# Layer 0's first keys ahead of other transfers, x loaded later, and unread products on TensorE at the start

## The chip, the cores and the metric

The kernel runs on one core of one Trainium2 chip. The metric is the device time of one execution in microseconds (us); the median of several executions is compared. Five engines work side by side and meet through semaphores: TensorE (PE, with its weight loads as PEld), VectorE (DVE), ScalarE (ACT), GpSimd (POOL) and SyncE (SP). Each engine runs its own queue in order. Loads are issued by instructions in the queues of SP and ACT and are carried out by 16 DMA engines.

## The reference

Four layers of a small transformer work on 32 sequences of 64 tokens of width 128, with a context of the same shape. Each layer adds a cross-attention block and a feed-forward block. Only layer 0's attention matters here. Cut to its core, with the context as the images and the normalised x as the latents:

```python
# x, ctx: (32, 64, 128); 16 heads of 64
img = layer_norm(ctx, ln1_g, ln1_b)
lat = layer_norm(layernorm(x), ln2_g, ln2_b)
q = lat @ Wq                                 # 64 queries a sequence
k, v = split(concat([img, lat]) @ Wkv)       # 128 keys a sequence
x = x + softmax(q @ k.T / 8) @ v @ Wo        # by head
```

After it come layer 0's feed-forward block with dequantised weights, and layers 1 to 3, which the change leaves as they are.

## The kernel before, in words

Layer 0's attention never forms the queries, keys and values. For each of the 16 heads it forms `A = Wq Wk^T / 8` (128x128) and `N = Wv Wo`. Then a sequence needs its 128 normalised tokens `kv_tok` (64 of the context, 64 of x, on the 128 partitions), their transpose `kvT`, the projection `G = A^T lat` (`l0_project`), scores `G kvT` with their softmax, the product with the tokens (`Ct`) and the sum over heads of `Ct N`, which is added to x.

The 32 sequences are taken as eight "quarters" `q` of four sequences (GT = 4). The change's title calls `q == 2` the third quarter. `l0_load` loads the tokens of one `q`: the context's half on SP's queue, x's half on ACT's. `l0_inputs` makes the keys: statistics (`ln_moments`, the helper's lines 154 and 155), a power on POOL (`rsqrt`, line 161), the normalisation (`ln_apply`, line 183), the gain (line 403) and the offset (line 404), four transposes (line 408), the copy to `kvT` (line 409), and two splits into a rounded part and its rest (`split`, lines 213 and 218): `latT_hi` and `latT_lo` of the latents' half of `kvT`, `tokp_hi` and `tokp_lo` of the tokens. Three rounded products in place of one (`mm3`, line 236) keep the precision.

`l0_products` multiplies pairs of weights for eight heads at a time (a half `hf`); `take_A` writes `A_hi` on ACT (line 364) and `A_lo` on DVE (line 365). `l0_project` multiplies `A` with `latT` for two heads per step `n`; the steps 0 to 3 need the half `hf = 0` only. `l0_unit` is one of 64 units: scores (line 445), maximum `nm` (line 447), exponentials, the normalisation on POOL (line 461), transposes (line 465), the split (468, 469), the product with the tokens, and for the last unit of a pair of sequences the sum over heads (479) and the addition to x (480). A unit of `q` also projects a step of `q + 1`, loads `q + 2` at its step 0 and makes its keys at step 2.

At the start the kernel loads quarter 0's tokens, WqT and WkT by halves, `gains`, quarter 1's tokens, WvT and Wo, then x in four groups of 256 KB (`K.x[g]`) and `cols`, a table of small bias columns. The first user of `cols` is `half_cols` (line 299), a scaled copy made by `later_constants`, which also makes `identb` and the mask `pair_mask`. The weights of the middle blocks are loaded by the task `mid_weights`, interleaved with the units.

The order in the text of the program is a priority only. The launch asks for a schedule made with a simulated timeline (`schedule_with_timeline_sim=True`): each engine's queue is laid out ahead of the run from simulated times, and on the chip it is worked off in that order, whatever arrives late. Two helpers restrict it: `in_turn(K, [a, b])` puts b behind a on their engine without waiting for a to end, and `tc.issue_after(a)` does the same for all that a block of the program issues on a's engine. A tile's buffer is used again when its readers are done: `kv_tok` has two buffers, so the load of quarter 2 waits for quarter 0's readers.

`keep_warm` issues products that nobody reads. Before the change it is called late in the kernel only, with the rounded identity `identb` as weights and a mask of the later layers, `K.masks[1]`, as the moving operand.

Of the kernel before, what the change touches and what calls it, by code (L numbers as in the profile page):

```python
# [4 lines left out]


# [3 lines left out]

# [8 lines left out]
F32 = mybir.dt.float32  # L19
F32R = mybir.dt.float32r  # L20
BF16 = mybir.dt.bfloat16
# [125 lines left out]
def ln_moments(K, pool, xg, own=""):  # L147

    nc = K.nc
    n = xg.shape[1]  # L150
    st = pool.tile([P, n, 6], F32, name="ln_st")
    mv = pool.tile([P, n, 2], F32, name=f"ln_mv{own}")
    for t in range(n):
        nc.vector.bn_stats(st[:, t, :], xg[:, t, :])
        nc.vector.bn_aggr(mv[:, t, :], st[:, t, :])
    return mv
# [51 lines left out]
def split(K, pool, src, name, engine=None, bufs=None, after=None):  # L208

    nc = K.nc  # L210
    hi = pool.tile(list(src.shape), F32R, name=f"{name}_hi", bufs=bufs)
    lo = pool.tile(list(src.shape), F32R, name=f"{name}_lo", bufs=bufs)
    first = nc.scalar.copy(hi, src) if isinstance(K, Later) else nc.vector.tensor_copy(hi, src)
    if after:
        in_turn(K, [after, first])
    if not isinstance(K, Later):
        K.mark = first
    (engine or nc.gpsimd).tensor_tensor(lo, src, hi.bitcast(F32), ALU.subtract)
    return hi, lo


# [61 lines left out]
def constants(K, pool):  # L283

    nc = K.nc
    K.ident = pool.tile([P, P], F32, name="ident")
    make_identity(nc, K.ident)
    K.neghalf = pool.tile([P, 1], F32, name="neghalf")
    nc.vector.memset(K.neghalf, -0.5)


def later_constants(K, pool):
    nc = K.nc
    K.identb = pool.tile([P, P], BF16, name="identb")
    nc.vector.tensor_copy(K.identb, K.ident)
    K.identr = pool.tile([P, P], F32R, name="identr")
    nc.vector.tensor_copy(K.identr, K.ident)
    K.half = pool.tile([P, NCOL], F32, name="half_cols")
    nc.vector.tensor_scalar(K.half, K.cols, 0.5, None, ALU.mult)

    K.pair_mask = pool.tile([P, GT, P], BF16, name="pair_mask")
    nc.vector.memset(K.pair_mask, NEG)
    for b in range(2):
        nc.vector.memset(K.pair_mask[b * S : (b + 1) * S, :, b * S : (b + 1) * S], 0.0)

    K.rank = pool.tile([P, 8], F32, name="rank")
    for e in range(8):
        nc.vector.memset(K.rank[:, e : e + 1], float(8 - e))
# [7 lines left out]
N_TAGS = "2n"  # L316


def l0_products(K, out, left, right, hf, tags=("s", "t")):


    ps = [bank(K, tag, [P, 4, P]) for tag in tags]
    for j in range(4):
        for r in range(2):
            rows = slice(r * S, (r + 1) * S)
            K.nc.tensor.matmul(ps[r][:, j, :], left[rows, 4 * hf + j, :], right[rows, 4 * hf + j, :], start=True, stop=True)
    for r in range(2):
        out(ps[r], hf, r)


def l0_xattn(K):


    nc, tc, ins = K.nc, K.tc, K.ins
    with (
        tc.tile_pool(name="l0x_w", bufs=1, reuse_waits="tile") as wp,
        tc.tile_pool(name="l0x_g", bufs=2, reuse_waits="tile") as gp,
        tc.tile_pool(name="l0x_t", bufs=L0_BUFS, reuse_waits="tile") as tp,
    ):
        C = SimpleNamespace(gp=gp, tp=tp, tok={}, keys={}, G={})  # L340

        C.A = tuple(wp.tile([P, 16, P], F32R, name=f"A_{n}") for n in ("hi", "lo"))
        C.N = wp.tile([P, 16, P], F32, name="N")
        with tc.tile_pool(name="first", bufs=1, side="right", reuse_waits="tile") as first:
            l0_load(K, C, 0)
            w = {n: first.tile([P, 8, P], F32, name=n) for n in ("WqT", "WkT", "WvT", "Wo")}
            from_dram = {n: ins[f"L0_xattn_{n}"].rearrange("(c p) d -> p c d", p=P) for n in w}
            half = [slice(4 * hf, 4 * hf + 4) for hf in range(2)]
            gains = wp.tile([P, 2, P], F32, name="gains")
            K.kv_gamma, K.kv_beta = gains[:, 0, :], gains[:, 1, :]  # L350
            for hf in range(2):
                nc.sync.dma_start(w["WqT"][:, half[hf], :], from_dram["WqT"][:, half[hf], :])
                nc.scalar.dma_start(w["WkT"][:, half[hf], :], from_dram["WkT"][:, half[hf], :])
                if hf == 0:
                    nc.sync.dma_start(gains, ins["gains"])
            l0_load(K, C, 1)
            nc.sync.dma_start(w["WvT"], from_dram["WvT"])
            nc.scalar.dma_start(w["Wo"], from_dram["Wo"])
            heads = lambda t, hf, r: t.rearrange("p (c r) d -> p r c d", r=2)[:, r, half[hf], :]

            def take_A(ps, hf, r):
                hi, lo = (heads(a, hf, r) for a in C.A)
                scale = 1.0 / math.sqrt(64.0)
                nc.scalar.activation(hi, ps, AF.Copy, scale=scale)
                nc.vector.scalar_tensor_tensor(lo, ps, scale, hi.bitcast(F32), ALU.mult, ALU.subtract)

            l0_inputs(K, C, 0)
            for hf in range(2):
                l0_products(K, take_A, w["WqT"], w["WkT"], hf)
                for n in range(4 * hf, 4 * hf + 4):  # L370
                    l0_project(K, C, 0, n, "gn"[n % 2])
            l0_inputs(K, C, 1)

            with tc.issue_after(K.projected.ins):
                for hf in range(2):
                    l0_products(K, lambda ps, hf, r: nc.scalar.copy(heads(C.N, hf, r), ps), w["WvT"], w["Wo"], hf, N_TAGS)
        for g in range(NG):
            K.x[g] = K.load(K.const, f"x{g}", [P, GT, P], K.tokens(ins["x"], g))
        K.cols = K.load(K.const, "cols", [P, NCOL], ins["cols"])
        mid_begin(K)  # L380
        units = [(q, t, hf, b) for q in range(8) for t in range(2) for hf in range(2) for b in range(2)]
        interleave(K, (Task(l0_unit(K, C, *u)) for u in units), L0_DEPTH, L0_LAG, L0_RATE)


def l0_load(K, C, q):
    tok = C.tok[q] = C.gp.tile([P, GT, P], F32, name="kv_tok")
    for rows, name, queue in ((slice(0, S), "ctx_1024", K.nc.sync), (slice(S, P), "x", K.nc.scalar)):
        batches = K.ins[name].rearrange("(b s) d -> s b d", s=S)
        queue.dma_start(tok[rows, :, :], batches[:, GT * q : GT * (q + 1), :])


def l0_inputs(K, C, q):

    nc, gp = K.nc, C.gp
    tok = C.tok[q]
    mv = ln_moments(K, gp, tok)
    rs = gp.tile([P, GT], F32, name="ln_rs")
    nc.vector.tensor_scalar(rs[0:S, :], mv[0:S, :, 1], EPS, None, ALU.add)
    nc.vector.tensor_scalar(rs[S:P, :], mv[S:P, :, 1], 1.0 + EPS, EPS * EPS, ALU.mult, ALU.add)
    ln_apply(K, tok, tok, mv, rsqrt(K, gp, rs, "ln_rstd"))  # L400
    full = [P, GT, P]
    engine = nc.vector if q == 0 else nc.gpsimd
    engine.tensor_tensor(tok, tok, K.kv_gamma.unsqueeze(1).to_broadcast(full), ALU.mult)
    engine.tensor_tensor(tok, tok, K.kv_beta.unsqueeze(1).to_broadcast(full), ALU.add)
    kvT = gp.tile(full, F32, name="kvT", bufs=3)
    ps = bank(K, "1", full)
    for b in range(GT):
        nc.tensor.transpose(ps[:, b, :], tok[:, b, :], K.ident)
    nc.scalar.copy(kvT, ps)
    latp = split(K, gp, kvT[:, :, S : 2 * S], "latT", nc.vector)  # L410
    tokp = split(K, gp, tok, "tokp", bufs=3)
    C.keys[q] = (kvT, latp, tokp)

# [14 lines left out]
def l0_unit(K, C, q, t, hf, b):  # L428
# [5 lines left out]
    G = C.G[q]  # L434
    if n == 0 and q + 2 < 8:
        l0_load(K, C, q + 2)
    if n == 2 and q + 2 < 8:
        l0_inputs(K, C, q + 2)
    if (hf, b) == (0, 0):
# [604 lines left out]
HEAD_BLOCKS = ("L2", "L3")  # L1044
WARM = ((0, 0, 0, 0), (0, 0, 2, 4))
WARM_END = 2


def heads_constants(K, pool):
# [318 lines left out]
def keep_warm(K, ps, n, after=None):  # L1368

    cols = ps.shape[-1]  # L1370
    moving = K.masks[1].rearrange("p h k -> p (h k)") if len(K.masks[1].shape) == 3 else K.masks[1]
    for _ in range(n):
        step = K.nc.tensor.matmul(ps, K.identb, moving[:, :cols], start=True, stop=True)
        if after is not None:
            in_turn(K, [after, step])
        after = step
    return after


def in_turn(K, steps):  # L1380

    for a, b in zip(steps, steps[1:]):
        order = mybir.DependencyInfo(mybir.DependencyClass.NoSync, mybir.DependencyReason.DATA)
        K.tc.add_manual_dep(b.ins, a.ins.name, order, reason="order of issue")
# [354 lines left out]
```

## Time and profile before

| | us |
|---|---|
| median of 3 runs | 907.39 |
| lowest and highest | 906.65 and 907.55 |
| the profiled execution | 907.62 |
| its span, first to last instruction | 905.9 |

| engine | busy us | share of the span |
|---|---|---|
| PE | 821.4 | 91% |
| PEld | 671.2 | 74% |
| DVE | 732.4 | 81% |
| ACT | 563.0 | 62% |
| POOL | 328.3 | 36% |

The mean granted TensorE clock of the execution is 0.98. In the timeline a row has the start and the duration in us, the engine, the line of the kernel, the operation, what it writes and reads, and the number of instructions merged into the row; in square brackets stands the idle time of the engine ahead of it and what ended that. A row of several instructions that overlap in a pipeline lasts less than their sum. Rows of "SPq" and "ACTq" are the queue of an engine: the issue of a load. Layer 0's attention takes the span from the start to about 320 us (its last sum over heads, line 479, starts at 319.5), with the middle blocks' groups between its units.

### The profile page before, as it was taken

What the parts mean: (1) busy time and instruction counts of PE and PEld (TensorE: products, weight loads), DVE (VectorE), ACT (ScalarE), POOL (GpSimd) and SP (SyncE); (2) the same over time, 40 slices, a digit from 0 to 9 for tenths busy, and PEclk for the clock granted to TensorE, in tenths of its full rate; (3) what the DMA queues carried; (4) which work ended last, traced back from release to release, by engine and by line L of the source; (5) the groups of instructions that cost most, each with busy time, mean ns of one, the idle gap of its engine ahead of it and who ended that gap; (6) DMA issues with size and microseconds to landing.
All of it is one profiled execution on the core that took longest, in us unless ns stands there. A gap on an engine that the chain in (4) does not pass through costs nothing.

```text
span 905.9 us, 15766 instructions
## 1 busy us (share of the span) xinstructions
PE 821.4 (91%) x5859; PEld 671.2 (74%) x5868; DVE 732.4 (81%) x1877; ACT 563.0 (62%) x1093; POOL 328.3 (36%) x300
## 2 busy tenths in 40 slices
PE   4999999999999988899999799898999779898995
PEld 3989989979988876787787688684676447566663
DVE  5879799798698687877678877789788778789878
ACT  3676685676676599587687768564544484345443
POOL 3764574343243251511040310015474303435342
PEclk9999999999999999999999999999999999899998
DMA  8312000000000000000000000000000000000000
GB/s 191 106 36 59 13 2 12 13 1 1 13 1 1 1 13 0 15 14 21 1 1 1 1 1 1 0 25 1 1 2 1 1 1 1 1 1 1 13 13 24
DMA packets 22670, 13.73 MB, mean 15 GB/s; under 512 B 3009, under 2 KB 21953, under 8 KB 22593
## 3 DMA queue, kind: packets, MB, share of 16 engines
q1 hardware_dynamic: 18320, 10.62, 4.3%
q10 hardware_dynamic: 4272, 2.10, 0.9%
q8 instruction: 46, 0.75, 0.3%
q14 instruction: 32, 0.25, 0.1%
HBM read 11.66 MB, written 1.05 MB: 14 GB/s over the span
## 4 chain that ended last, share of the span: by engine, by line
PE 50%; DVE 25%; ACT 15%; POOL 3%; issue 3%; DMA 2%; SPq 1%; ACTq 0%; DVEq 0%; POOLq 0%
PE c_ps L918 7%; PE g_ps L479 4%; PE s_ps L1263 4%; PE s_ps L445 4%; PE g_ps L236 4%; PE c_ps L236 3%; PE g_ps L1283 2%; PE c_ps L1273 2%; PE s_ps L236 2%; PE t_ps L465 2%; PE t_ps L236 2%; ACT L941 2%; DVE mh_lo L895 1%; ACT L936 1%; DVE m L893 1%
## 5 line engine op out<-in xcount | busy, mean ns | idle before, releaser
L461 POOL TENSOR_TENSOR e<-e,rs 128x512 f32<-128x512 f32 x64 | 67.0, 1058 | 91.7 <-DVE rs L460 52.8
L161 POOL TENSOR_TENSOR ln_rstd<-ln_rs,neghalf 128x4 f32<-128x4 f32 (+1 forms) x38 | 40.8, 1073 | 144.8 <-DVE ln_rs L169 137.5
L1249 POOL TENSOR_TENSOR kb<-hk,head 128x1024 f32<-128x1024 f32 x32 | 63.7, 1993 | 74.2 <-PE s_ps L1263 58.9
L445 PE MATMUL s_ps<-kvT,G 128*128 128x128 f32 x512 | 71.7, 277 | 0.5 <-DVE e L451 0.5
L1263 PE MATMUL s_ps<-kb,hq 128*128 128x512 f32 x128 | 67.3, 609 | 2.1 <-ACT hq L1232 1.9
L445 PEld LDWEIGHTS s_ps<-kvT,G 128*128 128x128 f32 x512 | 65.8, 192 | 4.1 <-DVE e L451 1.9
L918 PE MATMUL c_ps<-mh_hi,w2e_hi 128*128 128x512 f32 x160 | 61.8, 426 | 4.5 <-ACT be L936 2.7
L479 PE MATMUL g_ps<-N,Ct 128*128 128x128 f32 x512 | 62.1, 276 | 1.1 <-ACT G L425 0.7
L479 PEld LDWEIGHTS g_ps<-N,Ct 128*128 128x128 f32 x512 | 60.1, 192 | 2.5 <-ACT G L425 1.3
L1266 ACT ACTIVATE e<-e 128x1024 f32<-128x1024 f32 x32 | 34.0, 1061 | 40.6 <-DVE e L1265 38.1
L1264 DVE TENSOR_REDUCE nm<-s_ps 128x8 f32<-128x512 f32 x64 | 43.7, 683 | 16.0 <-PE s_ps L1263 15.6
L1274 ACT COPY hpT<-c_ps 128x512 f32<-128x512 f32 x64 | 35.1, 589 | 34.2 <-PE c_ps L1273 33.9
L469 DVE TENSOR_TENSOR pT_lo<-t_ps,pT_hi 128x512 fp32r<-128x512 f32 x64 | 43.4, 683 | 13.5 <-ACT pT_hi L468 11.3
L918 PE MATMUL c_ps<-mh_hi,w2e_lo 128*128 128x512 f32 x160 | 51.9, 401 | 0.0
L895 DVE TENSOR_TENSOR mh_lo<-m,mh_hi 128x1024 fp32r<-128x1024 f32 x32 | 40.4, 1263 | 13.9 <-ACT mh_hi L894 12.9
L473 ACT COPY Ct<-c_ps 128x512 f32<-128x512 f32 x64 | 38.4, 600 | 21.2 <-PE c_ps L236 16.4
L918 PE MATMUL c_ps<-mh_lo,w2e_hi 128*128 128x512 f32 x160 | 49.4, 404 | 0.5 <-DVE mh_lo L895 0.5
L425 ACT COPY G<-g_ps 128x512 f32<-128x512 f32 x60 | 35.9, 598 | 21.4 <-PE g_ps L236 18.0
L452 ACT ACTIVATE e<-e 128x512 f32<-128x512 f32 x56 | 35.4, 638 | 20.8 <-DVE e L451 20.5
L1283 PEld LDWEIGHTS g_ps<-hv,hpT 128*64 128x64 f32 x1024 | 33.5, 137 | 19.3 <-issue 7.4
L447 DVE TENSOR_REDUCE nm<-s_ps 128x4 f32<-128x512 f32 x64 | 42.9, 679 | 5.0 <-PE s_ps L445 4.7
L468 ACT CAST pT_hi<-t_ps 128x512 fp32r<-128x512 f32 x64 | 38.1, 598 | 13.3 <-PE t_ps L465 7.3
(524 smaller groups left out, 2651.8 us busy)
## 6 DMA issues: line engine op xcount, KB each, us to landing
kv_tok<-in_x ACTq DMA_DIRECT2D x8, 128.0 KB, 3.3
kv_tok<-in_ctx SPq DMA_DIRECT2D x8, 128.0 KB, 2.9
x<-in_x SPq DMA_DIRECT2D x4, 256.0 KB, 8.3
ctx<-in_ctx SPq DMA_DIRECT2D x4, 256.0 KB, 3.4
w2e_raw<-in_L_ffn_expert_w SPq DMA_DIRECT2D x1, 768.0 KB, 4.4
out<-x SPq DMA_DIRECT2D x3, 256.0 KB, 2.3
WkT<-in_L_xattn_WkT ACTq DMA_DIRECT2D x2, 256.0 KB, 5.3
WqT<-in_L_xattn_WqT SPq DMA_DIRECT2D x2, 256.0 KB, 5.2
```

The costliest lines, as they stand in the source:

```text
L236: step = K.nc.tensor.matmul(ps, w[a], x[b], start=start and i == 0, stop=stop and i == 2)
L445: nc.tensor.matmul(ps[:, j, :], G[:, bb, h : h + 2, :].rearrange("p h s -> p (h s)"), kvT[:, bb, :], start=True, stop=True)
L447: K.mark = nc.vector.tensor_reduce(nm, ps, AX.X, ALU.max, negate=True)
L461: nc.gpsimd.tensor_tensor(e, e, rs.unsqueeze(2).to_broadcast([P, 4, P]), ALU.mult)
L469: nc.vector.tensor_tensor(lo, ps, hi.bitcast(F32), ALU.subtract)
L479: nc.tensor.matmul(ps, Ct[:, h, :], C.N[:, h, :], start=(h == 0), stop=(h == 15))
L895: nc.vector.tensor_tensor(lo, m, hi.bitcast(F32), ALU.subtract)
L918: nc.tensor.matmul(ps, K.w2p[part][:, 2 * n + i, cols], x[:, i, :, :], start=first, stop=last)
L1249: step = nc.gpsimd.tensor_tensor(kb, K.hk[C.i][g][:, :, t, :].unsqueeze(2).to_broadcast(full), K.head.unsqueeze(1).unsqueeze(3).to_broadca ...
L1263: nc.tensor.matmul(ps, hq[:, half, t, :, :].rearrange("p b s -> p (b s)"), kb[:, half, :, :], start=False, stop=True)
L1264: nc.vector.tensor_reduce(nm[:, heads], ps, AX.X, ALU.max, negate=True)
L1283: values = nc.tensor.matmul(po[b * S : (b + 1) * S, j, :, :].rearrange("p r d -> p (r d)"), pT[:, j, b * S : (b + 1) * S], K.hv[g][:, 2 * ...
```

## The change

- `identb` and `pair_mask` are made by `constants`, at the start, instead of `later_constants`.
- Eight unread products (128x512) are issued on TensorE behind the start of the first load in the program's text, and six more in turn behind the first half of the `A` products. `keep_warm` now takes `pair_mask` as its moving operand everywhere.
- The first half of the `A` products stands ahead of quarter 0's inputs in the text; the second half is put, on PE's queue, behind quarter 0's transposes (`K.turn0`).
- Quarter 1's statistics, and `half_cols`, are put on DVE's queue behind quarter 0's `latT_lo` (`K.lat0`).
- `cols` is loaded ahead of WvT.
- The x part of quarter 2's load is issued on SP, like the context's.
- The four loads of x are issued on SP behind quarter 2's load, inside the first unit.

```diff
@@ split
-    (engine or nc.gpsimd).tensor_tensor(lo, src, hi.bitcast(F32), ALU.subtract)
+    K.split_end = (engine or nc.gpsimd).tensor_tensor(lo, src, hi.bitcast(F32), ALU.subtract)
@@ constants (moved here from later_constants)
+    K.identb = pool.tile([P, P], BF16, name="identb")
+    nc.vector.tensor_copy(K.identb, K.ident)
+    K.pair_mask = pool.tile([P, GT, P], BF16, name="pair_mask")
...
@@ later_constants
-    nc.vector.tensor_scalar(K.half, K.cols, 0.5, None, ALU.mult)
+    in_turn(K, [K.lat0, nc.vector.tensor_scalar(K.half, K.cols, 0.5, None, ALU.mult)])
@@ l0_products
+            step = K.nc.tensor.matmul(...)
+            if after is not None:
+                in_turn(K, [after, step])
...
+    return step
@@ l0_xattn
             l0_load(K, C, 0)
+            keep_warm(K, bank(K, "1", [P, 512]), WARM_START)
...
             l0_load(K, C, 1)
+            K.cols = K.load(K.const, "cols", [P, NCOL], ins["cols"])
             nc.sync.dma_start(w["WvT"], from_dram["WvT"])
...
+            step = l0_products(K, take_A, w["WqT"], w["WkT"], 0)
+            keep_warm(K, bank(K, "g", [P, 512]), 6, step)
             l0_inputs(K, C, 0)
             for hf in range(2):
-                l0_products(K, take_A, w["WqT"], w["WkT"], hf)
+                if hf:
+                    l0_products(K, take_A, w["WqT"], w["WkT"], hf, after=K.turn0)
                 for n in range(4 * hf, 4 * hf + 4):
                     l0_project(K, C, 0, n, "gn"[n % 2])
...
-        for g in range(NG):
-            K.x[g] = K.load(K.const, f"x{g}", [P, GT, P], K.tokens(ins["x"], g))
-        K.cols = K.load(K.const, "cols", [P, NCOL], ins["cols"])
@@ l0_load
-        queue.dma_start(tok[rows, :, :], batches[:, GT * q : GT * (q + 1), :])
+        K.tok_step = (queue if q != 2 else K.nc.sync).dma_start(tok[rows, :, :], batches[:, GT * q : GT * (q + 1), :])
@@ l0_inputs
-    mv = ln_moments(K, gp, tok)
+    with K.tc.issue_after(K.lat0.ins) if q == 1 else nullcontext():
+        mv = ln_moments(K, gp, tok)
...
-        nc.tensor.transpose(ps[:, b, :], tok[:, b, :], K.ident)
+        turn = nc.tensor.transpose(ps[:, b, :], tok[:, b, :], K.ident)
...
+    if q == 0:
+        K.turn0, K.lat0 = turn, K.split_end
@@ l0_unit
         l0_load(K, C, q + 2)
+        if q == 0:
+            for g in range(NG):
+                x = K.x[g] = K.const.tile([P, GT, P], F32, name=f"x{g}")
+                in_turn(K, [K.tok_step, K.nc.sync.dma_start(x, K.tokens(K.ins["x"], g))])
@@
+WARM_START = 8
@@ keep_warm
-    moving = K.masks[1].rearrange("p h k -> p (h k)") if len(K.masks[1].shape) == 3 else K.masks[1]
+    moving = K.pair_mask.rearrange("p t k -> p (t k)")
```

More of the change, by code (lines that the diff above doesn't have):

```diff
@@ L7 @@
 import math
-from contextlib import ExitStack
+from contextlib import ExitStack, nullcontext
 from types import SimpleNamespace
@@ L287, in constants @@
     make_identity(nc, K.ident)
+    K.identb = pool.tile([P, P], BF16, name="identb")
+    nc.vector.tensor_copy(K.identb, K.ident)
+    K.pair_mask = pool.tile([P, GT, P], BF16, name="pair_mask")
+    nc.vector.memset(K.pair_mask, NEG)
+    for b in range(2):
+        nc.vector.memset(K.pair_mask[b * S : (b + 1) * S, :, b * S : (b + 1) * S], 0.0)
     K.neghalf = pool.tile([P, 1], F32, name="neghalf")
@@ L293, in later_constants @@
     nc = K.nc
-    K.identb = pool.tile([P, P], BF16, name="identb")
-    nc.vector.tensor_copy(K.identb, K.ident)
     K.identr = pool.tile([P, P], F32R, name="identr")
@@ L298, in later_constants @@
     K.half = pool.tile([P, NCOL], F32, name="half_cols")
[L299 to L304, printed above, removed]
+    in_turn(K, [K.lat0, nc.vector.tensor_scalar(K.half, K.cols, 0.5, None, ALU.mult)])
     K.rank = pool.tile([P, 8], F32, name="rank")
@@ L316, with l0_products @@
 N_TAGS = "2n"
-def l0_products(K, out, left, right, hf, tags=("s", "t")):
+def l0_products(K, out, left, right, hf, tags=("s", "t"), after=None):
     ps = [bank(K, tag, [P, 4, P]) for tag in tags]
@@ L325, in l0_products @@
             rows = slice(r * S, (r + 1) * S)
-            K.nc.tensor.matmul(ps[r][:, j, :], left[rows, 4 * hf + j, :], right[rows, 4 * hf + j, :], start=True, stop=True)
+            step = K.nc.tensor.matmul(ps[r][:, j, :], left[rows, 4 * hf + j, :], right[rows, 4 * hf + j, :], start=True, stop=True)
+            if after is not None:
+                in_turn(K, [after, step])
     for r in range(2):
         out(ps[r], hf, r)
+    return step
 def l0_xattn(K):
```

## The prediction

> **What bounds the kernel now.** I read the page first (TensorE busy in 91% of the span, VectorE in 81%, and the chain that ended last running mostly through TensorE). Nothing in the change touches work after layer 0's first quarter, so I went on to the view of busy time by stretches:
>
> ```profile
> 5.00:10.00 5.00, 2.88 (x23) 2.65 (x25) 3.01 (x15) 4.28 (x5) 1.02 (x1) 1.00 1.18 281
> 10.00:15.00 5.00, 2.36 (x16) 1.70 (x14) 2.83 (x11) 1.23 (x3) 0.00 (x0) 1.00 1.22 271
> 15.00:20.00 5.00, 1.75 (x6) 1.46 (x7) 3.79 (x13) 0.64 (x2) 3.26 (x3) 1.00 0.56 119
> 20.00:25.00 5.00, 5.00 (x25) 4.88 (x24) 2.56 (x12) 2.00 (x4) 3.76 (x4) 1.00 0.19 50
> 25.00:30.00 5.00, 5.00 (x38) 4.60 (x37) 4.25 (x12) 2.54 (x5) 3.28 (x4) 1.00 0.19 56
> 30.00:35.00 5.00, 5.00 (x41) 4.81 (x42) 4.51 (x16) 4.25 (x15) 3.34 (x4) 1.00 0.37 100
> ...
> 100.00:150.00 50.00, 48.86 (x381) 45.54 (x381) 44.81 (x116) 31.90 (x64) 25.36 (x22) 1.00 0.04 12
> ```
>
> The columns are stretch and length, then busy us of PE, PEld, DVE, ACT and POOL, the granted clock, DMA share and GB/s. From 20 us on PE is full, with DVE at 90% behind it (44.81 of 50 at 100 to 150 us). Before 20 us nothing is full but the DMA (share above 1 from 5 to 15 us). So the program is a long stretch at the rate of PE and DVE behind a start of 18 us; what shortens the start should shorten the whole. Next, VectorE's rows in order of time:
>
> ```profile
> 8.55 0.69 DVE L403 TENSOR_TENSOR kv_tok<-kv_tok,gains 128x512 f32<-128x512 f32 x1
> 12.17 0.87 DVE L154 BATCH_NORM_STATS2 ln_st<-kv_tok 128x6 f32<-128x128 f32 x4 [2.93 <-DMA kv_tok<-in_ctx]
> 12.96 0.67 DVE L404 TENSOR_TENSOR kv_tok<-kv_tok,gains 128x512 f32<-128x512 f32 x1
> ...
> 17.50 0.19 DVE L299 TENSOR_SCALAR half_cols<-cols 128x49 f32<-128x49 f32 x1 [0.51 <-DMA cols<-in_cols]
> 17.61 0.28 DVE L213 CAST latT_hi<-kvT 128x256 fp32r<-128x256 f32 x1
> 17.97 1.12 DVE L183 TENSOR_SCALAR kv_tok<-kv_tok,ln_mv,ln_rstd 128x128 f32<-128x128 f32 x4
> 18.99 0.42 DVE L218 TENSOR_TENSOR latT_lo<-kvT,latT_hi 128x256 fp32r<-128x256 f32 x1
> 21.45 0.87 DVE L154 BATCH_NORM_STATS2 ln_st<-kv_tok 128x6 f32<-128x128 f32 x4 [2.03 <-DMA kv_tok<-in_ctx]
> ```
>
> Quarter 0 needs only its beta addition (L404) before its transposes, but the statistics of quarter 1 stand ahead of it in the queue and wait 2.93 us for their tokens. Its keys (`kvT`) are copied by 15.44 us, but the cast to `latT_hi` stands behind both hf=1 `A_lo` and `half_cols`, which waits for `cols`; SyncE issued that only at 12.84, behind the four x loads, whose issue took from 6.30 to 12.80. Last, TensorE's rows:
>
> ```profile
> 17.95 0.58 PE L236 MATMUL g_ps<-latT_hi,A_hi 128*128 128x256 f32 x1 [3.13 <-DVE latT_hi L213]
> 20.28 0.41 PE L236 MATMUL g_ps<-latT_lo,A_hi 128*128 128x256 f32 x1
> 20.49 0.41 PE L236 MATMUL n_ps<-latT_lo,A_hi 128*128 128x256 f32 x1
> 25.38 0.41 PE L236 MATMUL n_ps<-latT_hi,A_lo 128*128 128x256 f32 x1
> 27.75 0.28 PE L236 MATMUL g_ps<-latT_lo,A_hi 128*128 128x256 f32 x1
> 27.86 0.28 PE L236 MATMUL g_ps<-latT_hi,A_hi 128*128 128x256 f32 x1
> ```
>
> The first projection starts at 17.95. Until about 25.7 like products start 0.21 us apart (20.28 to 20.49), afterwards 0.12 (27.75 to 27.86), while the granted clock reads 1.00 throughout: a second, slower rate that this column does not show. It ended 7.75 us after the stream began, 6.2 us after its last gap (before 19.47).
>
> **Part by part.** Quarter 0's keys. With quarter 1's statistics ordered behind `latT_lo`, L404 follows L403 at 9.24 and ends at 9.91 instead of 13.63: 3.7 us. Ahead of the transposes now stand the warm-up products. The like row of the trace (L1373, 128x512 bf16) shows 0.38 us for one and about 0.22 from start to start at the fast rate, so about 0.43 at the slow one. Eight from 3.4 us (`identb` is cast at 3.15 to 3.38) end at 6.85, costing the hf=0 products 0.4 us against 6.42; these keep their 2.1 us to about 8.9; six more end at 10.2 to 11.4, by the rate. The transposes thus start between 9.98 (tokens) and 11.4; I take 10.7, where the rate changes on the way. They take 0.66 (row at 31.00) to 1.12 us (row at 13.70), the copy 0.6, the cast 0.28: the first projection starts at about 12.4 (11.5 to 13.1) instead of 17.95. Gain 5.5 us.
>
> Before it DVE has room for the hf=0 `A_lo` (two of 0.66) and `tokp_hi` (0.41) between 9.91 and 12.0. The hf=1 products (about 1 us fast, 2.1 slow) go behind the transposes and delay the projection little, since it waits for the copy and cast; their `A_lo` go behind `latT_lo` as well as I read the queue.
>
> The slow rate. PE is now fed from 3.4 us on, so by the trace's 6.2 to 7.75 us it is fast from 9.6 to 11.2, before the first projection. Before, 17.95 to 25.7 was run slow, less a gap of 0.3: 7.4 us of work that takes 3.7 fast. The edit so offers PE 5.5 + 3.7 = 9.2 us.
>
> [...]
>
> DVE's share. The projection feeds units at 2.5 us of DVE each (four passes of some 0.6 apart), against 2.2 to 2.8 on PE, so DVE must follow. Between 9.24 and 40 us its idle rows sum to 7.9 us: 2.93 + 0.51 + 2.03 + 0.91 + 0.72 + 0.41 + 0.39. What remains after the change: about 0.5 waiting for `kvT`, some 2 on POOL's powers (1.02 to 1.25 each, rows L161) and quarter 2's tokens. POOL's two-operand passes now lie on different DVE rows: `latT_lo` took 0.42 alone and 1.45 beside L403, so another 0 to 1 us. That leaves 7.9 - 2.5 - 0.5 = about 5, with 4.4 to 5.4 as its ends. PE offers 9.2 and DVE 5; they alternate as the limit at 30 to 60 us (4.97 of DVE's 5.00 at 40 to 45, PE's full 5.00 at 30 to 40). I take 6.5.
>
> Loads. Without the x loads (1 MB) in the DMA between 6 and 13 us, quarter 1's tokens land before the 12.1 of now, and they are first wanted at 12.5. `cols` now precedes `WvT` on SyncE: one issue of 0.83, hidden since `WvT` is first read at 25.87 before, about 16 after. The x loads stand behind quarter 2's load, which waits for quarter 0's tile (`tokp_lo`, 1.3 us on POOL, to about 13.5). They then block SyncE for 1.7 us (four of 0.43) to 6.5; queued behind are quarter 3's load, which cannot start until quarter 1's tile is free at about 20 us (25.59 before), and the middle blocks' weights, which in the trace began at 32.38. x is first read in the addition at 59.73, so 8 us of landing is covered; without that cover each late us would be paid. The third quarter's ACT issue (0.60 us, behind an ACT wait of 2.95 in the row at 18.39) goes to SyncE: nothing was due on ACT then, but with the `G` copies early it would stand before them, so this keeps 0 to 3 us from being lost and adds no gain of its own. The mask read by the late warm-up products is another tile of the same shape: 0.
>
> Sum: the profiled execution took 907.62 us, its span 905.9 and 1.7 around it, 0.2 above the median 907.39. 907.6 - 6.5 = 901.1.
>
> **Rivals.** *PE alone counts*: DVE's queue is laid out anew and its waits close up; the whole 9.2 comes, less 0.5 for late units: 898.9; with the slow rate's end at its earliest and quarter 2's waits gone, 897. For it: PE at 5.00 from 20 to 40 us. Against: DVE's 4.97 after. *DVE takes it back*: two-operand contention and quarter 2's waits return, leaving about 3 (5 less the 2.03 now waited at 21.45): 904.6. *Hidden anyway*: the gain meets a date that does not move, such as the middle blocks' weights, whose chain (loads, casts, splits) runs from 39 to 75 us; layer 0's later units wait there, and less than 1.8 us remains: 907. Against: PE lost only 1.1 us from 40 to 60. *Slower*: the queues are laid out by a planner with simulated times, so POOL's place for the split of `w1e` may come before `e` products that PE needs. Now POOL waits 2.15 us for its DMA at 40.9. If layer 0 moves 6.5 earlier and this load, behind the x loads on SyncE, does not, the wait grows to 8.7; it decides above 6.5 us of growth, where PE has no other unit left. With a further 2.15 for the next raw tile (`w2e`): 909.5. Against: the load waits for layer 0's own buffers, which come free earlier too.
>
> **How the numbers follow.** My sum 0.46 (899.5 to 903.5 by its terms), PE alone 0.16, DVE 0.19, hidden 0.08, slower 0.11. A measurement tells about 0.2%, 1.8 us, from no change: the first three lie past it, so faster 0.81, same 0.08, slower 0.11. The range 896.5 to 906.3 leaves out the slower case, most of the hidden one and little at the lower end.
>
> **What would show it.** Right: no idle before L404, `latT_hi` cast before 13 us and the first L236 product at 11.5 to 13.1; products 0.12 apart from the first; the first `nm` reduction well before 30.16; PE's full stretches beginning by 13 us. Wrong: the first L236 after 15 us, or still 0.21 apart; ACT or DVE idle behind `WvT`, x or `cols`; or an early start with PE waiting for DVE between 15 and 60 us by more than 3 us.

## Result: the start is 6 us shorter, the whole no faster

| | before | after |
|---|---|---|
| median, 22 runs each (us) | 907.01 | 910.17 |
| ratio, 95% interval | 1 | 1.003 [1.0017, 1.0042] |
| the profiled execution (us) | 907.62 | 909.24 |
| its span (us), mean granted clock | 905.9, 0.980 | 907.5, 0.976 |
| DVE busy (us) | 732.4 | 739.7 |

The changed kernel is slower by about 0.3%, 2.7 us by the ratio. After's 22 runs lie between 904.78 us (mean granted clock 0.983) and 913.51 us (0.968), so a part of the 2.7 us may go with the granted clock, which differs from run to run.

Line numbers have moved: the projection is still L236 and the normalisation L183, but the gain and offset are now L410 and L411, `A_lo` is L370, the loads of tokens L394 and of x L450, the maximum `nm` L461.

TensorE's rows of after, in order of time:

```profile
11.88 0.36 PE L236 MATMUL g_ps<-latT_hi,A_hi 128*128 128x256 f32 x1 [0.18 <-PE t_ps L326]
12.43 0.28 PE L236 MATMUL g_ps<-latT_lo,A_hi 128*128 128x256 f32 x1
12.55 0.28 PE L236 MATMUL g_ps<-latT_hi,A_hi 128*128 128x256 f32 x1
...
20.37 0.58 PE L236 MATMUL g_ps<-latT_hi,A_lo 128*128 128x256 f32 x1 [1.89 <-DVE A_lo L370]
22.04 0.41 PE L236 MATMUL n_ps<-latT_hi,A_lo 128*128 128x256 f32 x1
22.25 0.41 PE L236 MATMUL n_ps<-latT_lo,A_hi 128*128 128x256 f32 x1
```

The first projection starts at 11.88 instead of 17.95 and runs at once with products 0.12 us apart (12.43 to 12.55). Then PE waits 1.89 us for an `A_lo`, and after the wait the products are 0.21 apart again (22.04 to 22.25). The busy time by stretches (the columns are those of the prediction's first view) shows the same:

```profile
10.00:15.00 5.00, 4.21 (x40) 3.68 (x40) 4.00 (x15) 2.84 (x6) 1.27 (x1) 1.00 0.91 177
15.00:20.00 5.00, 3.48 (x28) 3.02 (x26) 1.14 (x5) 1.76 (x3) 0.00 (x0) 1.00 0.54 153
20.00:25.00 5.00, 4.63 (x24) 4.40 (x24) 4.57 (x18) 1.17 (x2) 3.29 (x3) 0.66 0.49 141
...
45.00:50.00 5.00, 3.27 (x27) 2.87 (x26) 4.96 (x8) 1.57 (x4) 4.22 (x4) 1.00 0.36 89
```

From 10 to 15 us PE has 4.21 us of work where it had 2.36. From 15 to 20 DVE is nearly empty (1.14 of 5) and PE not full. From 20 to 25 the granted clock is 0.66: 3.4 us of these 5 at half rate. From 45 to 50 DVE is busy for 4.96 us but finishes only 8 instructions. VectorE's rows name both places:

```profile
9.08 0.69 DVE L411 TENSOR_TENSOR kv_tok<-kv_tok,gains 128x512 f32<-128x512 f32 x1
...
11.34 0.39 DVE L213 CAST latT_hi<-kvT 128x256 fp32r<-128x256 f32 x1
...
18.86 0.87 DVE L154 BATCH_NORM_STATS2 ln_st<-kv_tok 128x6 f32<-128x128 f32 x4 [4.59 <-DMA kv_tok<-in_x]
...
43.55 3.96 DVE L183 TENSOR_SCALAR kv_tok<-kv_tok,ln_mv,ln_rstd 128x128 f32<-128x128 f32 x4
47.44 0.15 DVE L405 TENSOR_SCALAR ln_rs<-ln_mv 64x4 f32<-64x4 f32 x1
47.60 1.28 DVE L406 TENSOR_SCALAR ln_rs<-ln_mv 64x4 f32<-64x4 f32 x1
```

The offset no longer waits and the cast to `latT_hi` is at 11.34, as intended. Then the statistics of quarter 2 wait 4.59 us for their tokens, with an `A_lo` that PE needs queued behind them. At 43.55 the four normalisation passes take 3.96 us, which took 1.12 at 17.97 in before; L406, on 64x4 elements, takes 1.28 us, and 0.17 elsewhere in the same trace.

**Where the lead went.** The table gives the end of some instructions in us after the start of the span.

| | before | after | difference |
|---|---|---|---|
| 1st `nm` | 30.81 | 25.38 | -5.4 |
| 5th `nm` | 45.41 | 37.12 | -8.3 |
| 9th `nm` | 54.72 | 56.13 | +1.4 |
| layer 0's last sum over heads | 319.88 | 321.74 | +1.9 |

All of the lead is gone by 56 us, and afterwards the kernels run nearly in parallel. A part of the -8.3 was never a lead: by the 5th `nm` the kernel before had normalised four sets of tokens beyond quarter 0's, the one after only two; by the 9th both had done four. The fair account is DVE's up to 60 us. Its busy time rose from 44.3 to 49.05 us, so it was idle 4.75 us less, close to the 5 forecast. But the time of its instructions above the median of the same instruction (added up over rows that exceed it by 0.15 us or more) rose from 3.1 to 8.2 us, by 5.1. The idle time that the change filled came back as longer passes.

**Why quarter 2's tokens came late.** SyncE's queue in after, and then in before:

```profile
7.39 0.37 SPq L362 DMA_DIRECT2D WvT<-in_L_xattn_WvT  x1
7.81 1.57 SPq L1608 DMA_DIRECT2D w_r<-in_L_ffn_w_r  x2
...
9.91 3.79 SPq L674 DMA_DIRECT2D w_h<-in_L_ffn_w_h  x4
14.19 0.50 SPq L697 DMA_DIRECT2D bs<-in_cols  x1
14.82 0.60 SPq L394 DMA_DIRECT2D kv_tok<-in_ctx  x1
```

```profile
13.71 0.91 SPq L1593 DMA_DIRECT2D w_r<-in_L_ffn_w_r  x2
...
15.14 2.51 SPq L660 DMA_DIRECT2D w_h<-in_L_ffn_w_h  x4
17.70 0.50 SPq L683 DMA_DIRECT2D bs<-in_cols  x1
18.32 0.59 SPq L389 DMA_DIRECT2D kv_tok<-in_ctx  x1
```

Small weights of the middle blocks (`w_r`, `w_h`, `bs`) stood between x and quarter 2's load in before. With x gone from its place they moved up into it: SyncE issues them from 7.81 to 14.7, still ahead of quarter 2's load. A part of this time is SyncE's own waiting. From 5 to 20 us its waits in after hold these two (us in all, times, longest):

```profile
SPq L674 <- DMA kv_tok<-in_ctx: 2.1, 1, 2.1
SPq L697 <- DMA WvT<-in_L_xattn_WvT: 0.5, 1, 0.5
```

So 2.1 of the 3.79 us of the `w_h` row are a wait for an earlier load of tokens to land; in before 0.9 of the 2.51 us are a wait for x. The small weights were in the way not only by being issued but by waiting in front of quarter 2's load. That load is 3.5 us earlier than before (14.82 for 18.32), while DVE reaches its statistics at 14.27, so DVE waits.

**Why the passes are long.** GpSimd's rows of after:

```profile
42.55 2.04 POOL L475 TENSOR_TENSOR e<-e,rs 128x512 f32<-128x512 f32 x2 [0.84 <-PE g_ps L236]
44.54 2.38 POOL L218 TENSOR_TENSOR w1e_lo<-w1e_raw,w1e_hi 128x1024 fp32r<-128x1024 f32 x1
47.59 1.26 POOL L410 TENSOR_TENSOR kv_tok<-kv_tok,gains 128x512 f32<-128x512 f32 x1 [0.67 <-DVE kv_tok L183]
```

The normalisation (43.55 to 47.51) lies beside two `e` passes and `w1e_lo`, which end at 46.92. Taken singly its four passes last 1.12, 2.41, 0.33 and 0.33 us, where 0.34 is usual: the first ends at 44.67, with the second `e` pass (44.59), the second at 47.00, with `w1e_lo`. L406 (47.60 to 48.88) lies beside L410 (47.59 to 48.85): a pass worth 0.17 us ended when POOL's did. In before POOL stood idle when the same normalisation came up. VectorE's row there, and POOL's next ones:

```profile
41.92 1.11 DVE L183 TENSOR_SCALAR kv_tok<-kv_tok,ln_mv,ln_rstd 128x128 f32<-128x128 f32 x4
```

```profile
43.16 1.28 POOL L403 TENSOR_TENSOR kv_tok<-kv_tok,gains 128x512 f32<-128x512 f32 x1 [2.15 <-DMA w1e_raw<-in_L_ffn_expert_w]
...
45.77 2.04 POOL L461 TENSOR_TENSOR e<-e,rs 128x512 f32<-128x512 f32 x2
48.47 2.39 POOL L218 TENSOR_TENSOR w1e_lo<-w1e_raw,w1e_hi 128x1024 fp32r<-128x1024 f32 x1 [0.67 <-ACT w1e_hi L213]
```

The row at 43.16 names the load of `w1e_raw`, but L403 does not read it. L403 reads the tokens that DVE's L183 had finished at 43.02, so POOL stood idle because its next instruction needed the normalisation itself. (In experiment 9, where POOL has no work on `w1e`, the row still shows these 2.15 us.) What differs in after is the order of POOL's queue: in before the gain and the offset (L403, L404) stand ahead of two `e` passes and `w1e_lo`; in after the `e` passes and `w1e_lo` stand ahead of the gain (L410), and they run while DVE normalises.

The three ends of after's long passes agree with a DVE pass that waits until a whole POOL instruction is over: 44.67 after POOL's 44.59, 47.00 after 46.92, 48.88 after 48.85. That is the author's reading of the rows; what the two engines would contend for is not shown.

Collisions of this kind are not new in after. In before the first of the four passes at 24.34 lasts 1.30 us, until 25.64, beside POOL's `tokp_lo` (24.29 to 25.56), and L399 at 37.72 lasts 1.04 us beside an `e` pass (37.70 to 38.74).

### The profile page after: what moved, and what is told of

The parts are those of the page before. It is cut to its first block, busy times and chain, and to the rows that moved or that the text cites. A ratio compares the mean times of both kernels' runs of the same rounds, so it can differ in the third digit from the quotient of the medians.

```text
span 907.5 us, 15802 instructions
## 1 busy us (share of the span) xinstructions
PE 824.7 (91%) x5873; PEld 670.4 (74%) x5882; DVE 739.7 (82%) x1877; ACT 563.4 (62%) x1093; POOL 328.0 (36%) x300
## 4 chain that ended last, share of the span: by engine, by line
PE 48%; DVE 28%; ACT 15%; issue 4%; POOL 3%; DMA 2%; SPq 0%; ACTq 0%; DVEq 0%; POOLq 0%
PE c_ps L932 6%; PE s_ps L1278 4%; PE g_ps L493 4%; PE s_ps L459 4%; PE c_ps L236 3%; PE g_ps L236 3%; PE g_ps L1298 2%; PE c_ps L1288 2%; PE s_ps L236 2%; PE t_ps L236 2%; PE t_ps L479 2%; ACT L955 2%; ACT L950 1%; DVE mh_lo L909 1%; DVE kv_tok L183 1%
## 5 line engine op out<-in xcount | busy, mean ns | idle before, releaser
L466 ACT ACTIVATE e<-e 128x512 f32<-128x512 f32 x56 | 35.3, 638 | 25.5 <-DVE e L465 23.7
L461 DVE TENSOR_REDUCE nm<-s_ps 128x4 f32<-128x512 f32 x64 | 42.9, 678 | 4.6 <-PE s_ps L459 4.4
L977 POOL TENSOR_TENSOR be<-be 128x256 f32<-128x256 f32 x16 | 16.9, 1057 | 80.6 <-DVE tg L982 80.0
```

The source lines that it names most:

```text
L461: K.mark = nc.vector.tensor_reduce(nm, ps, AX.X, ALU.max, negate=True)
```

## The experiments

Each ratio is to the kernel before in the same batch of runs, whose medians were 907.54, 907.19 and 907.51 us. A difference between two experiments is worked out from their ratios times 907. The theories were: late tokens of quarter 2 (A in the expectations), a full DVE whose passes last longer beside POOL's (B), and, as rivals, the worth of the unread products (the slow rate) and the order of the queues (C), which the planner lays out anew after most edits. Traces tell how far the order stays the same: between after and experiment 1, all through on the four other engines; between experiments 1 and 8 until about 46 us, between after and experiment 10, and before and experiment 9, until about 50; in experiments 2, 3, 5, 6, 7 and 11 DVE's is new from 14 to 18 us on.

**1. Hold the small weights behind x.** After, with `w_r`, `w_h`, `bs` and `wf` put behind the last x load on SyncE; the queues of the other engines are the same, instruction for instruction. `HELD` names `w_r1`, `w_r2`, `w_h2` and `wf1`; the loads of `w_h1` and `bs1` are put behind `K.x_step` in the same way.

```diff
@@ l0_unit
+                K.x_step = K.nc.sync.dma_start(x, K.tokens(K.ins["x"], g))
+                in_turn(K, [K.tok_step, K.x_step])
@@ load
+        if name in HELD:
+            in_turn(K, [K.x_step, step])
```

> The changed kernel with one thing added: the small weights of the middle blocks (w_r1, w_r2, w_h2, w_h1, bs1, wf1) are put on SyncE behind the x loads; the order on the four other engines is the changed kernel's, instruction for instruction. Theory A (the gain of the start is lost in the wait for quarter 2's tokens, whose load stood behind these weights): the 4.59 us wait of VectorE at 14.27 falls below 1.5 us, TensorE's half-rate stretch at 20 to 24 us goes, and the time falls 3 to 5 us under the changed kernel, to 905 to 907. [...] Theory C (the order further on decides): the time follows the order, which is the same, so it falls by what the wait gives, as in A.

Measured: 906.15 us, 0.9988 [0.9971, 1.0005], 3.8 us better than after. VectorE's rows:

```profile
15.85 0.87 DVE L154 BATCH_NORM_STATS2 ln_st<-kv_tok 128x6 f32<-128x128 f32 x4 [1.75 <-DMA kv_tok<-in_x]
...
40.55 4.00 DVE L183 TENSOR_SCALAR kv_tok<-kv_tok,ln_mv,ln_rstd 128x128 f32<-128x128 f32 x4
```

Quarter 2's load is issued at 11.56, the wait falls from 4.59 to 1.75 us, PE is full from 15 to 20, and no half rate follows at 20. Each `nm` of layer 0 ends 3.0 us earlier than in after (1st 22.38, 9th 53.17). So the small weights cost what the shifted queue suggests, and they are not the whole: the normalisation is as long as in after (4.00), and the lead of 11.3 us at the 5th `nm` is 1.55 at the 9th.

**2. Put quarter 2's statistics behind quarter 1's `latT_lo`.**

```diff
-    with K.tc.issue_after(K.lat0.ins) if q == 1 else nullcontext():
+    with K.tc.issue_after(K.lat0.ins) if q in (1, 2) else nullcontext():
```

(`K.lat0` is set for q = 0 and again for q = 1; `half_cols` keeps the first.)

> The changed kernel with quarter 2's statistics put behind quarter 1's latT_lo on VectorE, SyncE's queue not touched on purpose. Theory A: VectorE no longer stands before the late tokens, so the second A_lo and quarter 1's normalisation come 4 us earlier; TensorE has no gap of 1.9 us at 18.5; 905 to 907. Theory B: the start gains 4 us, but the units run into a full VectorE; 908 to 911. Theory C (the queues are laid out anew from here on, worth plus or minus 2 us): anything from 903 to 911, with the first 30 us as in A.

Measured: 910.38 us, 1.0027 [1.0015, 1.0038]. The first 30 us are better still (1st `nm` 9.6 us ahead of before, PE at 4.95 to 5.00 of 5 from 15 to 35), and all is given back: the next normalisation takes 4.85 us at 36.88 beside one `e` pass, an offset and `w1e_lo`; PE waits 4.1 us and then runs at half rate from 44.2 to 47.6 (granted clock 0.74 from 45 to 50). So a better start brought nothing here, with DVE's queue new from 14.6 us on.

**3 and 4. After without the 14 unread products; before with them** (and with `identb` and `pair_mask` made early).

```diff
-            keep_warm(K, bank(K, "1", [P, 512]), WARM_START)
...
-            keep_warm(K, bank(K, "g", [P, 512]), 6, step)
```

> The changed kernel without its 14 unread products. If the products carry the gain of the start (theory A's first half), L236 runs 0.21 us apart until 20 us or later and the time is 1 to 3 us over the changed kernel: 911 to 913. If TensorE's rate at the start is hidden by VectorE (theory B): within 1 us, 909 to 911.

> The kernel before with only the 14 unread products and the earlier identb and pair_mask. If TensorE's slow rate costs the time (my prediction's second term, 3.7 us of offer): L236 runs 0.12 apart from 18 us on and the time falls 1 to 3 us under before, 904 to 906. If VectorE bounds the start (theory B): within 1 us of before, 906 to 908.

Measured: 911.06 us, 1.0039 [1.0022, 1.0057] without them, 0.8 us worse than after, within what the two intervals leave open; 906.74 us, 0.9988 [0.9977, 1.0] for them alone. In before they could not act: PE has little to do from 13 us, and products are 0.21 apart again from 19.7 to 26.5. In experiment 3 the queues are new from 14 us on, so 0.8 us is not their worth alone. The unread products thus explain little of what after lost; its half rate from 20.3 to 23.7 came with the wait for the tokens and, in experiment 1, went with it.

**5, 6 and 7. The normalisation of quarters 1 to 7 on ACT**, in experiment 1, in before, and in experiment 2. This takes the pass off DVE, where it lay beside POOL's.

```diff
-    ln_apply(K, tok, tok, mv, rsqrt(K, gp, rs, "ln_rstd"))
+    rstd = rsqrt(K, gp, rs, "ln_rstd")
+    if q == 0:
+        ln_apply(K, tok, tok, mv, rstd)
+    else:
+        nc.vector.scalar_tensor_tensor(rs, mv[:, :, 0], -1.0, rstd, ALU.mult, ALU.mult)
+        for t in range(GT):
+            nc.scalar.activation(tok[:, t, :], tok[:, t, :], AF.Identity, bias=rs[:, t : t + 1], scale=rstd[:, t : t + 1])
```

> The kernel with the weights held back (e1_hold), and the four-part normalisation of quarters 1 to 7 (line 183, on VectorE, stretched to 4.00 and 2.22 us beside GpSimd's passes at 40 to 53 us) done on ScalarE instead. [...] Theory C (the order of the queues further on decides): the stretch goes, but the end moves by any amount from -2 to +2. Theory D (a date set by the middle blocks' weight chain): stretch goes, no gain, 905 to 907.

> The control to e5_hold_act: the kernel before with the same normalisation on ScalarE. Theory B: before has no stretched pass at 40 to 60 us and 3.1 us of it at 20 to 40, and VectorE is not full there, so the gain is 0 to 2 us: 905.5 to 907.5. [...]

> e2_stats2 (quarter 2's statistics behind quarter 1's latT_lo) with the normalisation of quarters 1 to 7 on ScalarE. There line 183 took 4.85 us at 36.9 beside three GpSimd passes, TensorE then had 0.89 of 5 us of work at 40 to 45, and its rate halved at 44.2 for 3.4 us. Theory B: this hole goes, the time falls 3 to 5 us under e2_stats2's 910.4, to 905 to 907.5. Theory C: the hole goes, the end stays within 2 us of 910.

Measured: 904.38 us (theory B had given 902 to 904), 0.9955 [0.9936, 0.9974]; 911.04 us, 1.0047 [1.0024, 1.0069]; 907.2 us, 0.9977 [0.9957, 0.9996]. On top of experiment 1 it brings 3.0 us, on top of experiment 2 4.5 us, while in before it costs 4.3. In experiment 5 layer 0's last sum ends at 314.77 for 318.72 in experiment 1, 4.0 us earlier, within the 3 to 5 us of theory B. But DVE's time above the medians from 40 to 60 us falls only from 5.1 to 3.3, where theory B had less than 2: the edit's own small DVE instruction (L411, 0.16 us as a rule) takes 2.14 at 44.66, beside `w1e_lo`. In experiment 7 the hole was to go and did not: PE has 1.58 us of work from 45 to 50, then 6.8 us at half rate, and layer 0 ends at 320.46, no earlier than in before, though its 9th `nm` (43.03) stands 11.7 us ahead.

The control missed its expectation of 905.5 to 907.5. Its 9th `nm` (53.53) is 1.2 us earlier than before's, its layer 0 ends 2.5 later (322.37), and the cause was not traced. That the edit pays only where the change has made the pass collide fits the theory, but the queues are new in all three, so it is not proof.

**8, 9 and 10. The split of `w1e` on DVE instead of POOL**, in experiment 1, in before, and in after. This takes POOL's 2.4 us pass away and adds the same work to DVE: an estimate of 1.3 us, as DVE takes 1.26 us in before for a pass of that shape (`mh_lo`, 128x1024).

```diff
-    return split(K, pool, raw, name, after=after)
+    return split(K, pool, raw, name, engine, after=after)
...
-    K.w1p = load_split(K, K.moe_1, "w1e", ..., tmp, "y", minus=1)
+    K.w1p = load_split(K, K.moe_1, "w1e", ..., tmp, "y", minus=1, engine=nc.vector)
```

> e1_hold with the split of w1e (2.38 us on GpSimd at 41.57, beside which line 183 stood) on VectorE. [...] Theory B: line 183 still waits for the e products and gains on GpSimd, but for 2.4 us less; net a gain of 0 to 2 us: 904 to 906. Theory C: within 2 us of e1_hold either way.

> The control to e8_hold_w1e (0.9926 of before): the kernel before with only the split of w1e on VectorE. Theory B (the w1e pass on GpSimd costs when VectorE is full and line 183 runs beside it, which the earlier start brings about): before runs line 183 at 41.92 in 1.11 us while GpSimd waits for the w1e transfer, so the move is worth 0 to 2 us: 905.5 to 907.5. If it falls to 902 or less, e8_hold_w1e owes its gain to the split alone and not to the start.

> The changed kernel, weights not held back, with the split of w1e on VectorE. Theories A and B add up: it lacks e8_hold_w1e's 3 to 4 us of tokens that come earlier, but has its 4 us at 40 to 53 us: 904 to 906.5. If it stays at 909 or more, the w1e pass matters only where the tokens come early.

| | `w1e` on POOL | `w1e` on DVE |
|---|---|---|
| before | 1 | 1.0027 [1.0011, 1.0044] (909.73 us) |
| after | 1.003 [1.0017, 1.0042] | 0.9944 [0.9921, 0.9967] (903.08 us) |
| after, small weights held | 0.9988 [0.9971, 1.0005] | 0.9926 [0.9908, 0.9943] (901.38 us) |

The same edit costs 2.4 us in before and brings 7.8 in after and 5.6 in experiment 1. All three lie outside what was expected (905.5 to 907.5, 904 to 906.5, 904 to 906): the cost in before and the gain in the other two are larger. VectorE's rows of experiment 8, and POOL's next ones:

```profile
40.23 1.89 DVE L183 TENSOR_SCALAR kv_tok<-kv_tok,ln_mv,ln_rstd 128x128 f32<-128x128 f32 x4
...
46.60 1.11 DVE L183 TENSOR_SCALAR kv_tok<-kv_tok,ln_mv,ln_rstd 128x128 f32<-128x128 f32 x4
```

```profile
39.23 2.04 POOL L476 TENSOR_TENSOR e<-e,rs 128x512 f32<-128x512 f32 x2 [0.84 <-PE g_ps L236]
42.20 1.28 POOL L410 TENSOR_TENSOR kv_tok<-kv_tok,gains 128x512 f32<-128x512 f32 x1 [0.93 <-DVE kv_tok L183]
```

Up to here the trace stands 0.3 us from experiment 1's. Without `w1e_lo` behind the `e` passes the normalisation takes 1.89 for 4.00 us; the next one, 2.22 in experiment 1, takes 1.11. DVE's time above the medians from 40 to 60 us falls from 5.1 to 1.9, and the 9th `nm` ends at 49.56 for 53.17. The first normalisation's 2.1 us (4.00 to 1.89) come at equal queues, so they are shown to be the price of `w1e_lo` beside it. Behind about 46 us the queues are new. Of the 5.6 us 3.2 are the stretch from 40 to 60; the rest comes later, and no run tells whether it is fewer collisions or the new order.

In after the gain is 7.8, though DVE's wait for quarter 2 is as long as without the edit (4.64): there too more than the stretch came back, and what the rest is stays open. In before the first `nm` of experiment 9 ends 1.07 us later (31.88 for 30.81) with the same queues, so a single pair of traces can differ by that much without a cause in the edit; layer 0 ends 4.0 later (323.91). The change of sign in the table fits the collisions with POOL's pass, then, but does not prove that all of it is theirs.

**11 and 12. Experiment 8 without the unread products; experiment 8 with the x loads back in their old place**, taken out of the first unit, with the small weights still behind quarter 2's load. The edit of 11 is that of 3; of 12:

```diff
@@ 12, l0_xattn, behind WvT
+            for g in range(NG):
+                K.x[g] = K.load(K.const, f"x{g}", [P, GT, P], K.tokens(ins["x"], g))
```

> e8_hold_w1e without the 14 unread products. If TensorE's rate at the start counts once nothing else stalls (my prediction's second term): first projections 0.21 us apart until 20 us, time 1 to 4 us over e8_hold_w1e, 902.5 to 905.5. If VectorE hides it: within 1 us of 901.4.

> e8_hold_w1e with the four x loads back ahead, behind WvT's load; the queues of TensorE and GpSimd stay the same, and VectorE's but for one step. Quarter 2's load then stands behind the x loads, which took SyncE from 6.30 to 12.80 before. Theory A: quarter 1's tokens (12.2 now) and quarter 2's (15.8 now) land later by 1 to 3 us together, time 1 to 3 us over e8_hold_w1e: 902.5 to 904.5. If the x loads hide (my prediction priced the move at nothing but earlier tokens): within 1 us of 901.4.

Measured: 907.45 us, 0.9993 [0.9977, 1.001], and 905.28 us, 0.9973 [0.9959, 0.9987]. Without the products 6.1 us are lost: the first projection starts at 13.41, and PE, with a gap of 1.51 us before 18.43, runs at half rate from 19.9 to 26.7 (granted clock 0.50 from 20 to 25). The queues are laid out anew there, so 6.1 is not the products' worth alone. Both lost more than expected (902.5 to 905.5, 902.5 to 904.5). With x early 4.3 us are lost, at queues that differ by one step of DVE until 612 us, and DVE waits again where it waited in after:

```profile
19.71 0.87 DVE L154 BATCH_NORM_STATS2 ln_st<-kv_tok 128x6 f32<-128x128 f32 x4 [4.34 <-DMA kv_tok<-in_x]
```

x ahead of quarter 2's load makes DVE wait 4.34 us, the small weights ahead of it 4.59; in experiment 8 the wait is 1.60. Here both `A_lo` stand ahead of the wait, so PE stays full from 15 to 20, but later it waits 3.55 us for DVE's `e`, until 27.11, and runs at half rate from 26.0 to 36.2 (granted clock 0.50 from 30 to 35). So moving x aside was worth having, but in the change as made the weights took its place.

## Why the prediction was wrong

The forecast was 901.1 us and faster; the result was 910.17 and slower. The steps in turn:

**Quarter 0's keys: right.** Forecast 12.4 (11.5 to 13.1) for the first projection, measured 11.88; the gain was 6.1 us for 5.5. The first products were 0.12 apart, as forecast. Of the signs listed, the offset, the cast before 13 us, the projection and the first `nm` came true; "PE's full stretches beginning by 13 us" did not. One sign of being wrong came too: between 15 and 60 us PE waited for DVE 1.9 us for `A_lo` and 2.9 for `e`, more than 3 together.

**The slow rate: ended earlier than the sum had it, and came back.** The sum had PE fast from 9.6 to 11.2 us, by before's 6.2 to 7.75 us of feeding. In after the hf=0 products are 0.11 us apart at 7.81, where the same products were 0.21 apart in before (6.76 to 6.97). The first projection, at 11.88, starts later than all of these, so this changed nothing. No run shows what the rate's earliest end adds to the 897 of *PE alone counts*; in after it had ended by 7.81.

**Loads: failed.** The prediction named quarter 3's load and the weights from 32.38 as what was "queued behind" on SyncE. The rows from 13.71 to 18.2 in before, eight small loads between `cols` and quarter 2's load, were overlooked, and with them the question what moves into a place left free. "Quarter 2's tokens" and POOL's powers together were given some 2 us of DVE's waits; the tokens alone took 4.59, and experiment 1 prices the error at 3.0 us in the trace and 3.8 in the time. With the wait the slow rate came back for 3.4 us; in the sum it was to be gone for good.

**DVE's share: failed at the passes beside POOL's.** DVE's idle time fell by 4.75 us, where "about 5" was forecast. The prediction saw POOL's passes beside DVE's (1.45 against 0.42 us) and priced this at "another 0 to 1 us"; the passes grew by 5.1 us, of which experiment 8 takes 2.1 back at equal queues. Before's trace had more such rows than the one used (1.30 us at 24.34, 1.04 at 37.72; 3.1 us above the medians up to 60 us), and one row shows what one pass lost, not how many will collide. POOL's 2.15 us of idle time at 40.9 were read as a wait for its DMA. It waited for DVE's normalisation, and with `w1e_lo` and two `e` passes queued ahead of the gain that idle time was gone. Experiments 5 to 10 fit this term; how much of the 5.1 us reached the whole time stays open.

**Rivals.** *DVE takes it back* had the right mechanism (contention and quarter 2's waits) with 3 us still left over. *Slower* named the right tile, the split of `w1e`, and that its place in POOL's queue might change, but had POOL wait longer for the load; in fact the planner put `w1e_lo` and two `e` passes ahead of the gain, and they ran beside DVE's passes. *Hidden anyway* was argued against with 1.1 us that PE lost from 40 to 60 us; the rows give 1.0.

**The unread products: no difference between after and experiment 3 that the runs could tell** (0.8 us), since DVE set the pace. They may count where the two other terms are gone: 6.1 us in experiment 11, new queues included.

With both failed terms largely repaired (1.60 us of waiting and 1.9 of longer passes are left) the change gives 901.38 us (experiment 8, 6.7 us by the ratio), near the 6.5 that the sum had without them. That agreement supports the early terms of the sum but does not prove each, and may in part be luck: experiment 8 has DVE do the `w1e` work as well, its queues are new behind some 46 us, and 2.4 us of its gain have no traced cause.

## What to carry to other kernels

When a transfer is moved out of an in-order queue, list what stands behind it up to the next load that someone waits for: that is what moves up, and it may be as long as what left. When idle time of one engine is to be filled, ask whose passes lengthened its own in the trace of before, and in which order that other engine's queue will stand: here a pass of 2.4 us that moved ahead in POOL's queue ran beside DVE's short ones. Where a row names a load as the end of a wait, see whether the instruction reads that load at all. A lead at one instruction is a gain only if both kernels have done the same work by then.

## What the runs showed of the hardware

- Some DVE passes beside POOL's lasted until POOL's instruction ended: L406, on 64x4 elements, 1.28 us for 0.17 beside a 1.26 us pass, and the four passes of L183, 1.11 together, 3.96 to 4.85 beside three POOL passes (experiment 2 the longest). Others kept their time in after: the reductions `rs` (0.65 at 42.38) and `nm` (0.68 at 42.95) beside the same `e` passes. What decides was not tested.
- The half rate came back after short gaps: 1.89 us without a product in after, then 3.4 us (20.3 to 23.7) at a granted clock of 0.50. PE had been busy for 1.58 of the 3.4 us ahead of it (16.9 to 20.3). The length of the gap alone does not decide: in experiment 11 a gap of 1.51 us was followed by 6.8 us at half rate, and in experiment 10 a gap of 1.94 us, before 20.23, by products 0.12 us apart (20.45 to 20.57) and no half rate. What else decides was not tested.
- Issuing four small `w_h` loads took SyncE 3.79 us in after and 2.51 in before; four x loads took 6.50 us in before, 2.96 in after and 2.25 in experiment 1. Of the `w_h` rows 2.1 and 0.9 us are waits for earlier loads to land. A duration taken from one place did not hold in another; what sets it was not tested.
